# First attention layer, batches 0 and 1: row maxima read from the PSUM banks, scores formed a second time, negated maxima added by TensorE

## The chip, the core and the metric

The kernel is one program on one core of a Trainium2 chip. Its time is the device time of one execution in microseconds (us), median over runs. [...]

## The reference, cut to what matters

Four layers are chained with residual additions: an attention over the sequence with shared queries, keys and values and a mask, a second attention with modulated normalisation, a long scan of 256 steps, and a recurrent cell. Everything is fp32. Only the first layer is touched:

```python
qh = q.reshape(B, T, NH, dk).transpose(0, 2, 1, 3)      # B=8, T=512, NH=8, dk=32
scores = scale * jnp.einsum('bhqd,bhkd->bhqk', qh, qh)
logits = (scores * cmask + (1.0 - cmask) * NEG) * rmask
attn = jax.nn.softmax(logits, axis=-1)
ctx = jnp.einsum('bhqk,bhkd->bhqd', attn, qh)
```

## The kernel before

**Units.** The first layer of a batch `b` is cut into eight units `(b, e, kc)`: `e` is one of two groups of four heads, `kc` one of four blocks of 128 keys. A unit is four score tiles of 128 keys x 512 queries, one per head of the group. Because queries and keys are the same projection, the score matrix is symmetric, and the maximum along a row is also the maximum of a column.

**What a unit goes through.** `scores0` lets TensorE form the four tiles in four PSUM banks (L224: contraction over 32 rows, so the four heads use four row strips of the array) and ScalarE copies them to the SBUF tile `sc` (L229, four copies). `maxima0` (L234) is one VectorE reduction over 128 x 2048 that writes four columns of the tile `mxp0`. When all four `kc` of a group are reduced, `rows0` transposes `mxp0` on TensorE (L241), copies the result to `mrow` (L243), writes it to DRAM in four small DMAs (L247) and reads it back, broadcast to all 128 partitions, as `bc` (L248, 1 MB). `weights0` (L252) is one VectorE subtraction of `bc` from `sc`, `exps0` (L256) one ScalarE exponential over 128 x 2048 whose bias is the key mask. `values0` (L267) multiplies with the values and with ones into two further banks; `weigh0` (L284, L285 on VectorE, then GpSimd) divides. `masked_out` (L294, L297) is the output projection of the batch.

**Order.** All of it is emitted by a hand-written loop over steps `g`, with no scheduler: in step `g`, batch `b` forms the scores of unit `i` at `g = 8b-4+i`, runs `rows0` at `g = 8b` and `8b+4` (the very first group at `g = -1`), forms the weights of unit `i` at `g = 8b+1+i` and the values at `g = 8b+2+i`. Within a step the order is `scores0`, `rows0`, `project` (L198), `values0`, `project_out` (L215), `modulate` (L322, L325), `weights0` and `exps0`, `mask` (L210), `weigh0`, `maxima0`, `masked_out`, `modulation` (L153, steps 3 to 6), `normalize` (L306 to L311, batch 0 in step 11) and `qkv` (L334, batch 0 from step 13). From step 20 the heads of the second layer run as well. That layer already uses the scheme that the change brings to the first: `maxima1` reduces out of the banks (L393), `weights1` forms the scores again (L407) and adds negated maxima with a matrix `pick` (L417), and the exponential reads the bank (L427).

**Banks.** `bank(...)` hands out the five PSUM banks of the pool `ps_s`, to scores, projections, transposes and `qkv` alike. A freed bank goes to the end of a queue: the next request takes the bank whose last reader comes earliest in the program, and TensorE waits there until that reader is done. The values have banks of their own.

Of the kernel before, what the change touches and what calls it, by code (L numbers as in the profile page):

```python
# [8 lines left out]
F32 = mybir.dt.float32  # L9
AF = mybir.ActivationFunctionType  # L10
ALU = mybir.AluOpType
AX = mybir.AxisListType
# [3 lines left out]
P = 128  # L16
# [9 lines left out]
def attention(ctx, tc, cst, x, cond, wqT, woT, w_emb, b_emb, g_norm, w_qkv, g_q, g_k, w_out, follow):  # L26
# [14 lines left out]
    nc = tc.nc  # L41
# [4 lines left out]
    DH = 32  # L46
    SC = 1.0 / math.sqrt(DH)
    U = 8

    wp = ctx.enter_context(tc.tile_pool(name="a_w", bufs=1))  # L50
    big = ctx.enter_context(tc.tile_pool(name="a_big", bufs=1))
# [9 lines left out]
    def bank(shape, name):  # L61
        return ps_s.tile(shape, F32, tag="s", name=name)
# [60 lines left out]
    mxp0 = fone.tile([P, P], F32, name="mxp0")  # L123
    mxp1 = wp.tile([P, P], F32, name="mxp1")

    pick = wp.tile([P, 2, P], F32, name="pick")
    nc.gpsimd.memset(pick, 0.0)
    for h in range(4):
        for q in range(2):
            nc.gpsimd.tensor_tensor(  # L130
                pick[:, q, :], pick[:, q, :], ident[:, 32 * h + q : 32 * h + q + 1].to_broadcast([P, P]), ALU.add
            )
# [55 lines left out]
        nc.vector.tensor_mul(out, pc[:, 0, :], r)  # L188


    qms, psqs, qtoks, means, scs, bcs, pc0s, ctxTs = {}, {}, {}, {}, {}, {}, {}, {}

    def project(b, e):
        if e == 0:
# [23 lines left out]
    def scores0(b, e, kc):  # L218

        qm = qms[b, e]  # L220
        ss = [bank([P, D], f"s0_{b}_{e}_{kc}_{h}") for h in range(4)]
        for h in range(4):
            r = 32 * h
            nc.tensor.matmul(  # L224
                ss[h], lhsT=qm[r : r + 32, kc * P : (kc + 1) * P], rhs=qm[r : r + 32, :], start=True, stop=True
            )
        sc = ftwo.tile([P, 4, D], F32, tag="sc", name=f"sc_{b}_{e}_{kc}", bufs=7)
        for h in range(4):
            nc.scalar.copy(sc[:, h, :], ss[h])  # L229
        scs[b, e, kc] = sc  # L230

    def maxima0(b, e, qc):

        nc.vector.tensor_reduce(  # L234
            mxp0.rearrange("p (h i) -> p h i", i=32)[:, :, qc], scs[b, e, qc], AX.X, ALU.max
        )

    def rows0(b, e):

        pt = bank([P, P], f"pm0_{b}_{e}")  # L240
        nc.tensor.transpose(pt, mxp0, ident)  # L241
        mrow = ftwo.tile([P, P], F32, tag="mrow", name=f"mrow0_{b}_{e}", bufs=1)
        nc.scalar.copy(mrow, pt)  # L243
        bc = bcs[b, e] = ftwo.tile([P, 4, D], F32, tag="bc", name=f"bc_{b}_{e}")
        row = dram.tile([4, D], F32, tag="row", name=f"row_{b}_{e}", bufs=2)
        for h in range(4):
            nc.sync.dma_start(row[h].rearrange("(q n) -> q n", n=P), mrow[32 * h : 32 * h + 4, :])  # L247
        nc.sync.dma_start(bc, row.rearrange("h n -> (h n)").partition_broadcast(P).rearrange("p (h n) -> p h n", h=4))  # L248

    def weights0(b, e, kc):  # L250
        sc = scs[b, e, kc]
        nc.vector.tensor_sub(sc, sc, bcs[b, e])  # L252

    def exps0(b, e, kc):
        sc = scs[b, e, kc]
        nc.scalar.activation(sc, sc, AF.Exp, bias=negT[:, kc, b : b + 1], scale=SC)  # L256

# [39 lines left out]
            nc.vector.tensor_add(xs[b][:, m, :], ps, xs[b][:, m, :])  # L297


    xhs, xnTs, qTs, kTs, vts, mrows1, exs1, oTs = {}, {}, {}, {}, {}, {}, {}, {}  # L300

    def normalize(b):
        ss = sm.tile([P, 2], F32, tag="ss", name=f"ss_{b}")
        xh = [line(f"xh_{b}_{m}") for m in range(2)]
        for m in range(2):
            nc.scalar.activation(xh[m], xs[b][:, m, :], AF.Square, accum_out=ss[:, m : m + 1])  # L306
        rr = sm.tile([P, 2], F32, tag="rr", name=f"rr_{b}")
        nc.gpsimd.tensor_scalar(rr, ss, 1.0 / D, EPS, ALU.mult, ALU.add)
        nc.gpsimd.tensor_tensor(rr, rr, mhalf[:, 0:2], ALU.pow)
        for m in range(2):  # L310
            nc.scalar.activation(xh[m], xs[b][:, m, :], AF.Copy, scale=rr[:, m : m + 1])  # L311
        xhs[b] = xh

    def modulate(b):
        xnT = xnTs[b] = big.tile([P, NJ, 256], F32, tag="xnT", name=f"xnT_{b}")
# [180 lines left out]
    def leave(kind):  # L496
        for key in [k for k in left if k[0] == kind]:
            yield *key[1:], left.pop(key)

    with tc.manual_schedule():  # L500
        for g in range(-5, OUT[-1][1] + 1):

            a0, v0 = at(g, -4, U), at(g, 2, U)
            w1, v1 = heads(g, 1), heads(g, 2)

            a1, early = heads(g, 1, range(B - 2)), heads(g, 0, range(B - 2, B))
            late = a1 is not None or heads(g, 0, range(B - 2)) is not None
            turns, turned = list(leave("qkv")), list(leave("qt"))
            if a1:
                maxima1(*a1)  # L510
                if v1:
                    values1(*v1)
                if a := due.pop("weigh", None):
                    weigh0(*a)
            elif a0:
                scores0(a0[0], a0[1] // 4, a0[1] % 4)
            if (a := at(g, -3, U)) and a[1] % 4 == 3 and g > 0 and not a1:
                rows0(a[0], a[1] // 4)

            pr = at(g, -5, 2)  # L520
            if pr and not late:
                project(*pr)
            if v0 and not late:
                values0(v0[0], v0[1] // 4, v0[1] % 4)
            for a in turned:
                project_out(*a)
            if g == OUT[-1][1]:
                cst["soon"]()
                scan_start(cst["pool"], nc, cst)
            if g - 1 in norms:  # L530
                modulate(norms.index(g - 1))
            if a1 and a0:
                scores0(a0[0], a0[1] // 4, a0[1] % 4)
            if (a := at(g, -3, U)) and a[1] % 4 == 3 and a1:
                rows0(a[0], a[1] // 4)
            if w1:
                rows1(*w1)
            if e0 := at(g, 1, U):
                weights0(e0[0], e0[1] // 4, e0[1] % 4)
                if not late:  # L540
                    exps0(e0[0], e0[1] // 4, e0[1] % 4)
            if pr and not late:
                mask(*pr)
            if v0 and not late and v0[1] % 4 == 3:
                weigh0(v0[0], v0[1] // 4)
            if a0 and a0[1] % 4 < 3:
                maxima0(a0[0], a0[1] // 4, a0[1] % 4)

            if pr and late:
                project(*pr)  # L550
                mask(*pr)
            if a := at(g, U + 2):
                masked_out(a[0])
            if 3 <= g < 7:
                modulation(2 * g - 6)
            if g == U:
                scale_shift()
                add_identity()
            if g in norms:
                normalize(norms.index(g))  # L560
            made = [(part, qkv(*part)) for part in parts.get(g, ())]
            for b in range(B):
                for half in range(2):
                    if OUT[b][half] == g:
                        modulated_out(b, half)
                    if OUT[b][half] == g and (b, half) == (B - 1, 0):
                        for s in range(4):
                            for m in range(NJ // 2):
                                drive_of(nc, cst["us"], cst["x2T"], cst["ubias"], 0, s, m)
            if a0 and a0[1] % 4 == 3:  # L570
                maxima0(a0[0], a0[1] // 4, 3)
            if g == -1:
                rows0(0, 0)
            for part, lines in made:
                if lines:
                    qkv_norm(*part, *lines)
                    left["qkv", *part] = lines[1]
            if not w1:
                for a in turns:
                    qkv_out(*a)  # L580
            if early:
                maxima1(*early)

            if v1 and not a1:
                values1(*v1)
            if w1:
                weights1(*w1)
                for a in turns:
                    qkv_out(*a)
            if e0 and late:  # L590
                exps0(e0[0], e0[1] // 4, e0[1] % 4)
            if v0 and late:
                values0(v0[0], v0[1] // 4, v0[1] % 4)
                if v0[1] % 4 == 3:
                    due["weigh"] = v0[0], v0[1] // 4
            if (a2 := at(g, -7)) and a2[0] > 1:
                load(a2[0])
            if g == -1:
                load_weights()
            if g == U * B + 2:  # L600
                first.close()
                follow()
                for (b, half), d in x2d.items():
                    nc.sync.dma_start(
                        cst["x2T"][:, 2 * half : 2 * half + 2, b, :], d.rearrange("p (m t) -> p m t", m=2)
                    )
# [645 lines left out]
```

## Time and profile before

| | us |
|---|---|
| median of 3 runs | 2793.96 (2788.45 to 2795.03) |
| profiled execution, device time | 2791.91 |
| its span in the profile | 2790.0 |
| TensorE busy | 2709.0 (97%) |
| VectorE busy | 2130.1 (76%) |
| ScalarE busy | 1665.1 (60%) |
| GpSimd busy | 1247.9 (45%) |

The attention layers take about the first quarter of the span, the scan and the recurrent cell the rest. The change concerns steps -4 to 16, the first 153 us. TensorE's share over the whole span says little about these: in the 78 us from the start of step 3 (42.21 us) to that of step 13 (120.31 us) it is busy for 59.01 us. In the rows below, a line such as L224 is a line of the kernel before; PE is TensorE, DVE is VectorE, ACT is ScalarE, POOL is GpSimd, SP the engine that issues the DMAs. In a timeline row the numbers are start, duration, then engine, line, operation and tile, and in brackets how long the engine had been idle and what ended that. An fp32 matmul counts as two instructions there.

### The profile page before, as it was taken

The page shows a single profiled execution, that of the slowest core. Times are in us where ns is not written, and L with a number is a line of the kernel's source. Part 1 is how long each engine was busy: PE and PEld are TensorE (multiplying, and loading weights), DVE is VectorE, ACT ScalarE, POOL GpSimd, SP SyncE. Part 2 cuts the span into 40 slices and gives each one's busy share as a digit, 9 for nine tenths or more (in the row PEclk, how much of TensorE's full clock was granted, in tenths as well). Part 3 has the DMA queues.
Part 4 walks back from the last instruction along what each step waited for, and adds up shares of the span by engine and source line. Part 5 has one row for each costly group of instructions (what it writes and reads, how often), then busy time and mean ns, then how long its engine had stood idle before and what let it go on. Part 6 is the DMA issues. An engine that isn't in the chain of part 4 may idle for free.

```text
span 2790.0 us, 168552 instructions
## 1 busy us (share of the span) xinstructions
PE 2709.0 (97%) x71862; PEld 2063.7 (74%) x71862; DVE 2130.1 (76%) x9290; ACT 1665.1 (60%) x8176; POOL 1247.9 (45%) x3605
## 2 busy tenths in 40 slices
PE   7799999999989999999999999999999999999999
PEld 3234445444567888888888888888888888888888
DVE  6767776775347888888888888888888888888887
ACT  5666666664336666666666666666666666666653
POOL 1144323433314555555555545555555555544554
PEclk8899999999999999999999999999999999999999
DMA  4111101110400000000000000000000000000000
GB/s 152 42 43 35 43 24 50 35 35 20 151 2 4 7 7 8 7 7 7 7 7 7 7 7 7 7 7 7 8 8 7 7 7 7 7 7 7 7 7 8
DMA packets 56819, 58.17 MB, mean 21 GB/s; under 512 B 42832, under 2 KB 46456, under 8 KB 54016
## 3 DMA queue, kind: packets, MB, share of 16 engines
q1 hardware_dynamic: 55984, 47.39, 5.3%
q8 instruction: 561, 9.19, 1.4%
q14 instruction: 194, 1.59, 0.2%
q10 hardware_dynamic: 80, 0.01, 0.0%
HBM read 40.15 MB, written 7.21 MB: 17 GB/s over the span
## 4 chain that ended last, share of the span: by engine, by line
PE 89%; ACT 5%; DVE 3%; POOL 2%; issue 1%; DMA 1%; SPq 0%; DVEq 0%; ACTq 0%; POOLq 0%
PE ic L821 36%; PE pg L852 16%; PE gi L834 8%; PE pn L852 8%; PE psqkv L334 6%; PE pc L267 3%; PE pc L177 2%; PE s L224 2%; PE psx L453 1%; PE s L407 1%; PE n L385 1%; PE pso L294 1%; ACT sc L229 1%; PE s L417 1%; ACT sc L256 1%; PE psq L198 1%
## 5 line engine op out<-in xcount | busy, mean ns | idle before, releaser
L821 PE MATMUL ic<-cT_sb,tT 128*8 128x128 f32 x32736 | 1086.9, 273 | 9.5 <-ACT tT L719 8.8
L821 PEld LDWEIGHTS ic<-cT_sb,tT 128*8 128x8 f32 x32736 | 758.2, 89 | 254.8 <-ACT tT L719 213.2
L719 ACT ACTIVATE tT<-qn 128x16 f32<-128x16 f32 x2046 | 439.6, 215 | 548.2 <-DVE qn L1150 510.7
L1141 DVE STREAM_TRANSPOSE icT<-ic 128x64 f32<-128x64 f32 x2048 | 504.6, 246 | 55.1 <-PE ic L821 31.6
L852 PE MATMUL pg<-whh_sb,hz 128*32 128x128 f32 x16064 | 534.1, 273 | 0.0
L816 POOL TENSOR_TENSOR W<-W,cx 128x128 f32<-128x128 f32 x765 | 297.6, 389 | 375.3 <-ACT cx L792 371.8
L852 PEld LDWEIGHTS pg<-whh_sb,hz 128*32 128x32 f32 x16064 | 451.1, 110 | 1.5 <-issue 0.8
L1150 DVE SCALAR_TENSOR_TENSOR qn<-icT,hqs 128x16 f32<-128x16 f32 x2048 | 350.0, 171 | 70.1
L806 POOL TENSOR_TENSOR W<-cx,us 128x128 f32<-128x128 f32 x255 | 116.7, 457 | 433.4 <-ACT cx L792 433.4
L834 PE MATMUL gi<-wih_sb,x3T 128*32 128x128 f32 x8256 | 275.0, 274 | 0.0
L852 PE MATMUL pn<-whh_sb,hz 128*32 128x128 f32 x8032 | 267.8, 273 | 0.0
L834 PEld LDWEIGHTS gi<-wih_sb,x3T 128*32 128x32 f32 x8256 | 224.2, 110 | 16.8 <-POOL x3T L1164 16.6
L852 PEld LDWEIGHTS pn<-whh_sb,hz 128*32 128x32 f32 x8032 | 226.0, 110 | 1.0 <-issue 0.5
L1098 DVE SCALAR_TENSOR_TENSOR sqmm<-sqmm,qn 128x32 f32<-128x32 f32 x768 | 142.8, 186 | 97.6 <-ACT sqmm L1081 97.5
L1107 DVE TENSOR_TENSOR hqs<-W,sqmm 128x32 f32<-128x32 f32 x1020 | 194.7, 191 | 18.6 <-DVE sqmm L1098 0.5
L792 ACT ACTIVATE cx<-qn 128x32 f32<-128x32 f32 x1280 | 200.6, 213 | 0.0
L792 ACT ACTIVATE cx<-p 128x32 f32<-128x32 f32 x1020 | 149.9, 217 | 53.5 <-DVE p L1093 53.5
L334 PE MATMUL psqkv<-wqkv_sb,xnT 128*128 128x512 f32 x384 | 175.5, 603 | 3.8 <-ACT sc L229 3.1
L234 DVE TENSOR_REDUCE mxp<-sc 128x4 f32<-128x2048 f32 x64 | 145.9, 2282 | 26.4 <-ACT sc L229 26.2
L393 DVE TENSOR_REDUCE mxp<-n 128x2 f32<-128x512 f32 x128 | 79.5, 683 | 109.9 <-PE n L385 109.9
L229 ACT COPY sc<-s 128x512 f32<-128x512 f32 x256 | 131.4, 608 | 42.2 <-PE s L224 42.2
L252 DVE TENSOR_TENSOR sc<-sc,bc 128x2048 f32<-128x2048 f32 x64 | 147.5, 2305 | 11.7 <-DMA bc<-row 11.7
(176 smaller groups left out, 3875.3 us busy)
## 6 DMA issues: line engine op xcount, KB each, us to landing
bc<-row SPq DMA_DIRECT2D x16, 1024.0 KB
out<-o SPq DMA_DIRECT2D x1008, 4.0 KB
x<-in_x SPq DMA_DIRECT2D x8, 512.0 KB
wqkv_sb<-in_L_cond_W_qkv SPq DMA_DIRECT2D x1, 3072.0 KB
wih_sb<-in_L_cond_W_ih SPq DMA_DIRECT2D x4, 768.0 KB
whh_sb<-in_L_cond_W_hh SPq DMA_DIRECT2D x4, 768.0 KB
x2d<-x2o SPq DMA_DIRECT2D x11, 256.0 KB
x2T<-x2d SPq DMA_DIRECT2D x11, 256.0 KB
```

The costliest lines, as they stand in the source:

```text
L229: nc.scalar.copy(sc[:, h, :], ss[h])
L252: nc.vector.tensor_sub(sc, sc, bcs[b, e])
L334: nc.tensor.matmul(ps, lhsT=xnTs[b][:, c, m * P : (m + 1) * P], rhs=wqkv_sb[:, c, part * D : (part + 1) * D], start=(c == 0), stop=(c == N ...
L719: seen["tanh"] = nc.scalar.activation(tT, src[:, half * HM : (half + 1) * HM, :], AF.Tanh)
L792: a = nc.scalar.activation(c[:, i], x, AF.Copy, scale=f)
L816: seen["sum"] = nc.gpsimd.tensor_tensor(W[:, i + 1 : 5], W[:, i + 1 : 5], c, ALU.add)
L821: last = nc.tensor.matmul(ps[32 * j : 32 * j + B, :], lhsT=tT[k // HM][:, k % HM, :], rhs=cT_sb[:, k, 0, :, j, :], start=(k == 0), stop=(k ...
L834: nc.tensor.matmul(gi_ps[rows(j), g, :], lhsT=x3T[c][:, k, :], rhs=wih_sb[:, k, g, :, j, :], start=(k == 0), stop=(k == NJ - 1),)
L852: nc.tensor.matmul((pg_ps, pg_ps, pn_ps)[g][rows(j), :], lhsT=hzs[tau % 3][:, k, 32 * (g % 2) : 32 * (g % 2) + 32], rhs=whh_sb[:, k, g, :, ...
L1107: nc.vector.tensor_sub(hq, W[:, s], mm)
L1141: turn = nc.vector.transpose(icT.rearrange("p m n -> p (m n)"), ic[:, half * 64 : half * 64 + 64])
L1150: stt(qn[:, m2, :], icT[:, :, 0:B], IC[s], hq[:, m2, :], ALU.mult, ALU.add)
```

## The change

For batches 0 and 1 (`DIRECT = 2`):

- `scores0` no longer copies; VectorE reduces each of the four banks straight into a column of `mxp0`. These reductions stand at the place of `scores0`, at the head of the step, while the one of `maxima0` stood near its end.
- `rows0` ends with a ScalarE copy scaled by -1 into `nrow`; the DRAM round trip is gone.
- `weights0` asks for four banks again, forms the scores again and adds `-max` with 16 small matmuls (`pick` gets four planes instead of two); ScalarE takes the exponential from the banks, four times 128 x 512.
- `maxima0` and `exps0` do nothing for these batches. `mrow` has two buffers.
- `normalize` of batch 0 is split: the two scaled copies stand at the head of step 12 instead of in step 11.

```diff
+    DIRECT = 2
...
-    pick = wp.tile([P, 2, P], F32, name="pick")
+    pick = wp.tile([P, 4, P], F32, name="pick")
...
-        for q in range(2):
+        for q in range(4):
...
     def scores0(b, e, kc):
...
+        if b < DIRECT:
+            for h in range(4):
+                nc.vector.tensor_reduce(mxp0[:, 32 * h + kc : 32 * h + kc + 1], ss[h], AX.X, ALU.max)
+            return
...
     def rows0(b, e):
...
+        if b < DIRECT:
+            nrows[b, e] = ftwo.tile([P, P], F32, tag="mrow", name=f"nrow_{b}_{e}", bufs=2)
+            nc.scalar.activation(nrows[b, e], pt, AF.Copy, scale=-1.0)
+            return
...
     def weights0(b, e, kc):
+        if b < DIRECT:
+            qm, nrow = qms[b, e], nrows[b, e]
+            ss = [bank([P, D], f"w0_{b}_{e}_{kc}_{h}") for h in range(4)]
+            for h in range(4):
+                r = 32 * h
+                nc.tensor.matmul(
+                    ss[h], lhsT=qm[r : r + 32, kc * P : (kc + 1) * P], rhs=qm[r : r + 32, :], start=True, stop=False
+                )
+            for q in range(4):
+                for h in range(4):
+                    r = 32 * h
+                    nc.tensor.matmul(
+                        ss[h][:, q * P : (q + 1) * P],
+                        lhsT=pick[r : r + 4, q, :],
+                        rhs=nrow[r : r + 4, :],
+                        start=False,
+                        stop=(q == 3),
+                    )
+            sc = scs[b, e, kc] = ftwo.tile([P, 4, D], F32, tag="sc", name=f"sc_{b}_{e}_{kc}", bufs=7)
+            for h in range(4):
+                nc.scalar.activation(sc[:, h, :], ss[h], AF.Exp, bias=negT[:, kc, b : b + 1], scale=SC)
+            return
...
     def normalize(b):
...
+        if b > 0:
+            normalized(b)
+
+    def normalized(b):
         for m in range(2):
-            nc.scalar.activation(xh[m], xs[b][:, m, :], AF.Copy, scale=rr[:, m : m + 1])
+            nc.scalar.activation(xhs[b][m], xs[b][:, m, :], AF.Copy, scale=rrs[b][:, m : m + 1])
...
+            if g - 1 == norms[0]:
+                normalized(0)
```

More of the change, by code (lines that the diff above doesn't have):

```diff
@@ L188, in weigh @@
         nc.vector.tensor_mul(out, pc[:, 0, :], r)
-    qms, psqs, qtoks, means, scs, bcs, pc0s, ctxTs = {}, {}, {}, {}, {}, {}, {}, {}
+    qms, psqs, qtoks, means, scs, bcs, nrows, pc0s, ctxTs = {}, {}, {}, {}, {}, {}, {}, {}, {}
     def project(b, e):
@@ L241, in rows0 @@
         nc.tensor.transpose(pt, mxp0, ident)
-        mrow = ftwo.tile([P, P], F32, tag="mrow", name=f"mrow0_{b}_{e}", bufs=1)
+        if b < DIRECT:
+            nrows[b, e] = ftwo.tile([P, P], F32, tag="mrow", name=f"nrow_{b}_{e}", bufs=2)
+            nc.scalar.activation(nrows[b, e], pt, AF.Copy, scale=-1.0)
+            return
+        mrow = ftwo.tile([P, P], F32, tag="mrow", name=f"mrow0_{b}_{e}", bufs=2)
         nc.scalar.copy(mrow, pt)
@@ L250, in weights0 @@
     def weights0(b, e, kc):
+        if b < DIRECT:
+            qm, nrow = qms[b, e], nrows[b, e]
[18 more added lines that the diff above has]
+                nc.scalar.activation(sc[:, h, :], ss[h], AF.Exp, bias=negT[:, kc, b : b + 1], scale=SC)
+            return
         sc = scs[b, e, kc]
@@ L254, in exps0 @@
     def exps0(b, e, kc):
+        if b < DIRECT:
+            return
         sc = scs[b, e, kc]
@@ L297, in masked_out @@
             nc.vector.tensor_add(xs[b][:, m, :], ps, xs[b][:, m, :])
-    xhs, xnTs, qTs, kTs, vts, mrows1, exs1, oTs = {}, {}, {}, {}, {}, {}, {}, {}
+    rrs, xhs, xnTs, qTs, kTs, vts, mrows1, exs1, oTs = {}, {}, {}, {}, {}, {}, {}, {}, {}
     def normalize(b):
@@ L309, in normalize @@
         nc.gpsimd.tensor_tensor(rr, rr, mhalf[:, 0:2], ALU.pow)
+        xhs[b] = xh
+        rrs[b] = rr
+        if b > 0:
+            normalized(b)
+    def normalized(b):
         for m in range(2):
-            nc.scalar.activation(xh[m], xs[b][:, m, :], AF.Copy, scale=rr[:, m : m + 1])
-        xhs[b] = xh
+            nc.scalar.activation(xhs[b][m], xs[b][:, m, :], AF.Copy, scale=rrs[b][:, m : m + 1])
     def modulate(b):
```

## The prediction

> **What bounds the kernel now.** I read the chain of work that ended last over the first 300 us, then the waits of the first 200 us, the timeline of steps -4 to 18, and for prices the groups by shape and the second layer, which already works in the new way.
>
> The chain shows two regimes. Up to step 12 it runs through DMA round trips and whatever VectorE has to do behind them; from step 13 it is TensorE alone:
>
> ```profile
> 29.59 4.63 DMA bc<-row
> ...
> 54.86 4.69 DMA bc<-row
> ...
> 82.17 5.06 DMA bc<-row
> 87.25 2.29 DVE sc L252
> ...
> 138.05 1.07 PE s L224 x8
> 139.12 1.85 PE pc L267 x16
> 140.98 3.65 PE psqkv L334 x8
> ```
>
> The last three rows add to 6.57 us, and that is a whole step: scores start at 137.98 (step 15) and 144.54 (step 16). There every matmul added lengthens the step. The timeline gives the start of the scores in steps 3 to 17: 42.2, 49.2, 57.0, 62.2, 71.5, 76.5, 79.7, 83.7, 100.8, 106.3, 120.3, 131.4, 138.0, 144.5, 153.0.
>
> The waits say what the round trip costs: 10.6 us of VectorE idle in five waits, of which batches 0 and 1 have four (0.91, 3.00, 3.73, 1.26 in the timeline, sum 8.9). TensorE's longest wait is a consequence, for VectorE is late with `weigh0`:
>
> ```profile
> DVE sc L252 <- DMA bc<-row: 10.6, 5, 3.7
> PE pc L267 <- DVE ctxT L285: 12.0, 2, 9.1
> ```
>
> From 42.2 to 120.3 us (steps 3 to 12) the busy times by window give TensorE 59.0 of 78.1 us: 19.1 us idle.
>
> **Prices.** Groups of the page (mean ns is the figure after the busy time):
>
> ```profile
> L234 DVE TENSOR_REDUCE mxp<-sc 128x4 f32<-128x2048 f32 x64 | 145.9, 2282 | 26.4 <-ACT sc L229 26.2
> L393 DVE TENSOR_REDUCE mxp<-n 128x2 f32<-128x512 f32 x128 | 79.5, 683 | 109.9 <-PE n L385 109.9
> L229 ACT COPY sc<-s 128x512 f32<-128x512 f32 x256 | 131.4, 608 | 42.2 <-PE s L224 42.2
> L252 DVE TENSOR_TENSOR sc<-sc,bc 128x2048 f32<-128x2048 f32 x64 | 147.5, 2305 | 11.7 <-DMA bc<-row 11.7
> ```
>
> The second layer, first as the chain, then as the timeline:
>
> ```profile
> 668.85 0.65 PE s L407 x8
> 669.49 0.45 PE s L417 x16
> ```
>
> ```profile
> 670.90 2.06 ACT L427 ACTIVATE ex<-s 128x512 f32<-128x512 f32 x4 [1.43 <-PE s L417]
> 673.77 2.49 DVE L393 TENSOR_REDUCE mxp<-n 128x2 f32<-128x512 f32 x4 [3.54 <-PE n L385]
> 676.31 0.33 PE L397 MATMUL pm<-ident,mxp 128*128 128x128 f32 x1 [0.69 <-DVE mxp L393]
> ```
>
> Per unit the change removes four copies (2.05 us in a row at 131 us) and an exponential of 2.00 from ScalarE, and gives it four exponentials (2.06, second row): -2.0. VectorE loses 2.28 + 2.31 and gets four reductions from the banks, 2.49 in a row: -2.1. TensorE gets a second score block, 1.07, and 16 small matmuls: eight took 0.45 (chain row), so 0.90. Four rows of `pick` instead of two is not in the trace; if the strips did not overlap it would be 16 times two 0.27 us rows, 8.6, but L417 shows them overlapped, so 0.90, and twice that at the half clock. Together +1.97 for each of 16 units.
>
> At no cost: eight more `pick` additions on GpSimd (2.89 us for eight now, over by 9.3 us, first use near 32 us). The 20 DMAs go from SP's queue, so `wqkv_sb` and `wout_sb`, queued behind the first `bc` at 29.98, leave earlier; their cover is that they are first read in step 13 and step 8. Without it they would delay `x` of batch 1, needed at 43 us; that one is queued ahead. The split `normalize` leaves ScalarE's order as it was, as nothing of ScalarE stands between the two places.
>
> **The new waits.** Now each unit passes the five banks twice, and what TensorE waits for is read off the order of requests.
>
> Scores behind weights. In steps without other work behind `weights0`, the next scores get banks that the exponentials still read. The third one ends 0.1 + 3 x 0.515 = 1.65 us after the last small matmul. A late bank costs a full matmul more:
>
> ```profile
> 100.78 1.83 PE L224 MATMUL s<-qm 32*128 32x512 f32 x8
> 101.50 0.29 PEld L224 LDWEIGHTS s<-qm 32*128 32x128 f32 x2 [0.41 <-DVE x L297]
> ```
>
> From 101.50 to 102.61 is 1.11. So such scores end 2.75 after, instead of 1.07: +1.7 in steps 3, 8, 9, 10; where it is the fourth exponential, +2.2 in steps 12 and 13, +0.3 in step 5.
>
> `rows0` behind reductions. In steps 4 and 8 the four reductions of the next group are issued ahead of the transposition of `mxp0`, which they write too. TensorE waits for them in order, and `project` and `values0` stand behind it: +2.5 (2.49 above) in step 4, and 0.7 in step 8, where the staggered scores hide the rest.
>
> `modulation` in step 3 asks for the banks of exponentials just issued: +1.2.
>
> Step by step, from the TensorE rows (scores 1.07, values 1.85, weights 1.97, projection 1.95, transposes 0.6, `modulation` 1.86, `masked_out` 3.63) and these waits:
>
> - step 3: 2.75 + 1.95 + 1.85 + 1.97 + 1.2 + 1.86 + 0.1 = 11.7 (6.9 before); 4: 12.2 (7.8); 5: 7.7 (5.2); 6: 6.9 (9.4); 7: 5.0 (4.9)
> - step 8: 2.75 + 0.7 + 0.33 + 1.85 + 1.97 = 7.6 (3.3); 9: 6.6 (4.0); 10: 10.2 (17.1); 11: 6.9 (5.5)
> - step 12: 19.0 (14.0). `normalize` stays exposed: the exponentials now end 2.2 into the step, squares 1.3, GpSimd 2.9, the copies to the projection's bank 1.85, then as before 7.2 to the end of the transposes (the projection at half clock, 3.78), 1.65 for `xnT`, whose banks the weights get, 1.1 and 0.9.
>
> Sum 93.8 against 78.1: **+15.7**. Checked from the other side: without any wait the TensorE rows of these steps add to 71.7, so 22.1 of it are waits.
>
> Steps 13 to 16: +0.2 (step 13 was slow before, at half clock), +2.0, +2.0, +1.0 (a wait for GpSimd of 0.84 in step 16 is covered): **+5.2**.
>
> Start: 16 reductions in a row end at 24.8 instead of 26.4, and no round trip follows, but scores and weights take turns in the banks: step 3 starts at 39.8 at full clock, 43.2 at half (the window 30 to 40 us shows 0.50 now), taken 41.5: **-0.7**, bounds -2.4 and +1.0.
>
> Sum +20.2. Nothing after step 17 differs, and its waits are relative to TensorE's place, so it is carried to the end: 2791.91 + 20.2 = 2812.1. The median stands 2.05 above the profiled execution: **2814**.
>
> **The clock.** The rows show the half rate after idle times:
>
> ```profile
> 81.84 1.06 PE L267 MATMUL pc<-sc,qtok 128*32 128x512 f32 x8 [0.94 <-ACT sc L256]
> 93.94 1.94 PE L267 MATMUL pc<-sc,qtok 128*32 128x512 f32 x8 [9.10 <-DVE ctxT L285]
> 123.90 1.86 PE L267 MATMUL pc<-sc,qtok 128*32 128x512 f32 x8 [1.68 <-ACT sc L256]
> ```
>
> 0.94 leaves full speed, 1.68 does not, and one such episode costs 1.4 to 1.8 us (3.5 to 3.8 for the pair of rows instead of 2.1; 3.78 instead of 1.98 for a projection). The new waits of 1.7 to 2.5 lie on that edge. I leave them at full clock, since work on both sides is dense.
>
> [...]
>
> **Rivals.**
> - *Clock falls at each bank wait.* 1.6 us in steps 3, 4, 5, 8, 9, 10 and 1.7 at the start: +11.3, **2825**. For: 123.90; against: 81.84.
> - *Engines run ahead.* ScalarE and VectorE have spare time, so two thirds of the 22.1 us of waits vanish: -14.7, **2799**. For: their busy time falls by 2 us a unit; against: TensorE's order is fixed and the bank needs its reader.
> - *Faster: the added matmuls fall into TensorE's idle time.* 10 units add 19.7 us in steps 3 to 12, where 19.1 are idle. If they fit, the round trip's 8.9 and the half-clock excess 8.1 go, and 5.2 of steps 13 to 16 stay: -11.8, **2782**. It decides if steps 7 to 9 stay near 5 us, that is if scores need not wait for exponentials. Against: five banks for eight tiles.
>
> **Numbers.** Forecast 0.66, clock 0.12, running ahead 0.13, faster 0.09. Range 2791 to 2832: from below the second rival to above the clock one with the start at its bad end. A measurement here tells 0.3%, 8.4 us, from no change: faster 0.09, same 0.13, slower 0.78.
>
> **What would show it.** Right: scores of step 17 near 173 us; steps 8 and 9 near 7 us, with L225 waiting for ScalarE's L282; in step 4 the transposition waiting 2.5 us for VectorE; steps 14 and 15 at 8.5. Wrong: step 3 to 13 in less than 80 us, or 14 and 15 still at 6.6.

## The result, and the profile after

The changed kernel takes 2824.66 us (median of 4 runs, 2823.02 to 2834.99); before, beside it, took 2791.65 (2788.45 to 2795.03). The ratio is 1.0131, 95% interval 1.0115 to 1.0148: it is slower, by 33 us by the medians and 37 by the ratio, where 20 were forecast. The profiled span is 2821.2 us, 31.2 more than before's 2790.0. From here on "step n" is the stretch from the start of step n's scores to that of step n+1.

On the page, TensorE has 50.9 us more busy time than before, of which 31.5 were forecast as added rows; VectorE has 31 less.

```profile
PE 2759.9 (98%) x72502; PEld 2095.9 (74%) x72502; DVE 2099.1 (74%) x9322; ACT 1642.6 (58%) x8160; POOL 1250.1 (44%) x3613
```

In the waits of the first 200 us (engine, line, what it waited for, total, times, longest) the two round-trip lines that the prediction showed are gone. ScalarE and VectorE now wait for TensorE's matmuls, and TensorE waits for VectorE's reductions, in step 4 for 2.65 us:

```profile
ACT sc L282 <- PE w L273: 54.2, 15, 9.5
DVE mxp L230 <- PE s L225: 36.0, 15, 5.3
...
PE pm L248 <- DVE mxp L230: 5.3, 3, 2.6
```

The chain that ended last (start, length, what), formerly DMA and VectorE up to step 12, is TensorE nearly throughout. The first four rows are the end of step 9 and the start of step 10: second scores, small matmuls, and then scores that last 3.09 instead of 1.07 us, because they wait for banks that the exponentials still read. The last five are step 15, the old 6.57 us plus 1.07 and 0.89:

```profile
105.19 1.07 PE w L267 x8
106.26 0.89 PE w L273 x32
107.15 3.09 PE s L225 x8
110.25 1.85 PE pc L302 x16
...
163.92 1.07 PE s L225 x8
164.99 1.85 PE pc L302 x16
166.84 1.07 PE w L267 x8
167.91 0.89 PE w L273 x32
168.81 3.64 PE psqkv L374 x8
```

Step 4 in the timeline (start, duration, line, tile; in brackets the idle time and what ended it) shows the costliest stretch. Scores run at half speed (2.09), the transposition waits 2.65 us for the last reduction, and the projection behind it is still at half speed (3.62 instead of 1.98):

```profile
53.90 2.09 PE L225 MATMUL s<-qm 32*128 32x512 f32 x8
56.01 2.49 DVE L230 TENSOR_REDUCE mxp<-s 128x1 f32<-128x512 f32 x4 [3.97 <-PE s L225]
58.64 0.44 PE L248 MATMUL pm<-ident,mxp 128*128 128x128 f32 x1 [2.65 <-DVE mxp L230]
58.88 3.62 PE L199 MATMUL psq<-x,wq_sb 128*128 128x512 f32 x4
```

The clock had already fallen when that wait began. Windows of 1 us (length, then the busy share of TensorE, of its weight loads, of VectorE, ScalarE and GpSimd; the granted clock is the third number from the end) put the fall at 53.3 us. A second one follows at 70.4 us, where TensorE has been counted busy without a pause since 58.6:

```profile
53.00:54.00 1.00, 1.00 (x11) 0.98 (x10) 0.00 (x0) 0.28 (x1) 0.00 (x0) 0.64 0.00 0
70.00:71.00 1.00, 1.00 (x9) 0.27 (x8) 0.00 (x0) 0.40 (x1) 0.00 (x0) 0.68 0.00 0
```

| stretch | before | forecast | after |
|---|---|---|---|
| start of step 3 | 42.21 | 41.5 | 41.90 |
| steps 3 to 12 | 78.10 | 93.8 | 100.06 |
| of these: 4, 5, 8 | 7.84, 5.20, 3.25 | 12.2, 7.7, 7.6 | 16.1, 9.0, 9.4 |
| steps 13 to 16 | 32.70 | 37.9 | 39.78 |
| start of step 17 | 153.01 | 173.2 | 181.74 |

### The profile page after: what moved, and what is told of

It is laid out like the page before. It is cut to its first block, busy times and chain, and to the rows that moved or that the text cites. A ratio compares the mean times of both kernels' runs of the same rounds, so it can differ in the third digit from the quotient of the medians.

```text
span 2821.2 us, 169835 instructions
## 1 busy us (share of the span) xinstructions
PE 2759.9 (98%) x72502; PEld 2095.9 (74%) x72502; DVE 2099.1 (74%) x9322; ACT 1642.6 (58%) x8160; POOL 1250.1 (44%) x3613
## 4 chain that ended last, share of the span: by engine, by line
PE 91%; ACT 4%; DVE 3%; POOL 1%; issue 1%; DMA 0%; SPq 0%; DVEq 0%; ACTq 0%; POOLq 0%
PE ic L863 35%; PE pg L894 15%; PE gi L876 8%; PE pn L894 8%; PE psqkv L374 6%; PE pc L302 4%; PE s L225 3%; PE pc L178 2%; PE psx L493 1%; PE s L447 1%; PE n L425 1%; PE s L457 1%; PE pso L329 1%; PE psq L199 1%; ACT sc L234 1%
## 5 line engine op out<-in xcount | busy, mean ns | idle before, releaser
L863 PE MATMUL ic<-cT_sb,tT 128*8 128x128 f32 x32736 | 1086.0, 273 | 9.9 <-ACT tT L761 9.1
L863 PEld LDWEIGHTS ic<-cT_sb,tT 128*8 128x8 f32 x32736 | 757.6, 89 | 255.9 <-ACT tT L761 215.4
L876 PEld LDWEIGHTS gi<-wih_sb,x3T 128*32 128x32 f32 x8256 | 224.2, 110 | 17.6 <-POOL x3T L1206 17.6
L834 ACT ACTIVATE cx<-q 128x32 f32<-128x32 f32 x1020 | 145.6, 213 | 0.0
L1123 ACT ACTIVATE sqmm<-qn 128x32 f32<-128x32 f32 x768 | 140.3, 183 | 0.0
L374 PEld LDWEIGHTS psqkv<-wqkv_sb,xnT 128*128 128x128 f32 x384 | 70.4, 191 | 91.5 <-issue 75.5
```

What stands on the lines that cost most here:

```text
L374: nc.tensor.matmul(ps, lhsT=xnTs[b][:, c, m * P : (m + 1) * P], rhs=wqkv_sb[:, c, part * D : (part + 1) * D], start=(c == 0), stop=(c == N ...
L834: a = nc.scalar.activation(c[:, i], x, AF.Copy, scale=f)
L863: last = nc.tensor.matmul(ps[32 * j : 32 * j + B, :], lhsT=tT[k // HM][:, k % HM, :], rhs=cT_sb[:, k, 0, :, j, :], start=(k == 0), stop=(k ...
L876: nc.tensor.matmul(gi_ps[rows(j), g, :], lhsT=x3T[c][:, k, :], rhs=wih_sb[:, k, g, :, j, :], start=(k == 0), stop=(k == NJ - 1),)
L1123: nc.scalar.activation(sq, qs, AF.Square, scale=math.sqrt(CUB[s]))
```

## The experiments

All ratios are to the kernel before. Beside each stands the start of step 17 in its one profiled execution; from there to the end the kernels are alike, but the stretch took 2633.2 to 2640.7 us in the traces, so a single span is not good to better than some us.

| run | ratio (95%) | median us | step 17 at |
|---|---|---|---|
| before | 1 | 2787.5 to 2791.7 | 153.0 |
| after | 1.0131 (1.0115 to 1.0148) | 2824.66 | 181.7 |
| e1 matmuls added, unread | 1.0084 (1.0069 to 1.0099) | 2812.96 | 172.6 |
| e2 no round trip | 0.9986 (0.9976 to 0.9996) | 2785.27 | 151.8 |
| e3 both | 1.0058 (1.0043 to 1.0073) | 2804.61 | 167.2 |
| e4 second tile of maxima | 1.0131 (1.0116 to 1.0146) | 2826.42 | 190.7 |
| e5 sums behind second scores | 1.0135 (1.0113 to 1.0157) | 2828.75 | 192.2 |
| e6 no small matmuls | 1.0054 (1.0036 to 1.0073) | 2805.30 | 167.1 |
| e7 e4, `modulation` in halves | 1.0134 (1.0116 to 1.0152) | 2827.54 | 192.7 |
| e8 three orders | 1.0117 (1.0099 to 1.0134) | 2822.57 | 180.0 |
| e9 one unit only | 0.9979 (0.9971 to 0.9988) | 2782.02 | 147.0 |
| e10 first blocks only | 1.0001 (0.9992 to 1.0010) | 2788.33 | 153.3 |
| e11 two orders | 1.0091 (1.0077 to 1.0105) | 2812.61 | 176.6 |
| e12 fillers | 1.0117 (1.0100 to 1.0134) | 2820.60 | 188.5 |

**The parts by themselves (e1, e2, e3).** e1 puts the second scores and small matmuls of the same shapes into before, at the place of `weights0`, into banks that nothing reads:

```diff
     def weights0(b, e, kc):
+        if b < 2:
+            qm = qms[b, e]
+            ss = [bank([P, D], f"w0_{b}_{e}_{kc}_{h}") for h in range(4)]
...
         sc = scs[b, e, kc]
         nc.vector.tensor_sub(sc, sc, bcs[b, e])
```

> The kernel before, with the added TensorE work of the change but without its handover: for batches 0 and 1 the second score block and the 16 small matmuls are issued at the place of the weights into four banks that nobody reads; everything else is as before. Theory A (banks changing hands, the ordered wait for the reductions and the half clock make most of the loss; the matmuls themselves fall largely into TensorE's idle time): +2 in each of steps 3 and 4, +7 in steps 13 to 16, nearly nothing in steps 5 to 12, in all +9 to +15 us against before. Rival B (the 16 x 1.97 = 31.5 us of added matmuls are the loss, since that is about what was measured): +28 to +33 us.

The ratio makes 23 us (0.0084 x 2789) of 31.5 us of rows, between the ranges of theory A and rival B and in neither. In steps 3 to 12 it is 15.2 of the ten units' 19.7 (93.33 against 78.10 us): only 4.5 vanish in idle time. TensorE's longest wait is still there, merely cut from 9.10 to 4.95 us, since its end is set by `bc` and then by VectorE's queue, neither of which the rows touch:

```profile
95.85 2.29 DVE L252 TENSOR_TENSOR sc<-sc,bc 128x2048 f32<-128x2048 f32 x1 [3.17 <-DMA bc<-row]
...
102.53 1.94 PE L285 MATMUL pc<-sc,qtok 128*32 128x512 f32 x8 [4.95 <-DVE ctxT L303]
```

e2 leaves the round trip out and subtracts a constant tile:

```diff
+        if b < 2:
+            if (b, e) == (0, 0):
+                bcs[0, 0] = fixed = ftwo.tile([P, 4, D], F32, tag="bc", name="bc_fixed")
+                nc.gpsimd.memset(fixed, 0.0)
+            bcs[b, e] = bcs[0, 0]
+            return
```

> The kernel before, without the DRAM round trip of the maxima for batches 0 and 1: the subtraction takes a constant tile, so the subtracted maxima are left out there; reductions, transposition and the copy to mrow stay. It prices what the change could win at most by dropping the trip. Theory A: the exposed 8.9 us of VectorE waits go, and part of the half-clock excess: -9 to -17 us against before. Rival C (the trip is hidden behind the chain of VectorE and TensorE, another wait takes its place): 0 to -4 us.

It gives 4 us (1 to 7), as rival C has it, where VectorE had waited 8.9. In step 9 the subtraction no longer waits, yet `weigh0` is still behind it, and step 10's values wait 5.17 us for VectorE instead of 9.10:

```profile
83.97 2.29 DVE L258 TENSOR_TENSOR sc<-sc,bc_fixed 128x2048 f32<-128x2048 f32 x1
...
86.17 1.75 DVE L290 RECIPROCAL r<-pc 128x256 f32<-128x256 f32 x1
...
90.64 1.93 PE L273 MATMUL pc<-sc,qtok 128*32 128x512 f32 x8 [5.17 <-DVE ctxT L291]
```

e3 is both edits at once.

> Both of the two others at once: no round trip (maxima not subtracted for batches 0 and 1) and the added matmuls into unread banks. This has the TensorE work of the changed kernel and no DMA wait, but ScalarE and VectorE work as before and no bank that must be read before TensorE goes on with the second block. Theory A: between -4 and +8 us against before, some 25 to 35 below the changed kernel. Rival B: +20 us or more, near the changed kernel.

16 us (12 to 20), again between theory and rival. So of the change's 37 us by ratio, 16 are there without any reader on the new banks. By subtraction about 20 are left for the readers: reductions and exponentials from banks, the handover, and what falls of the clock come with them.

**The small matmuls (e6).** Without them the maxima are not subtracted:

```diff
-            for q in range(4):
-                for h in range(4):
-                    r = 32 * h
-                    nc.tensor.matmul(
-                        ss[h][:, q * P : (q + 1) * P],
...
```

> The changed kernel without the 16 small matmuls of each unit: the maxima are not subtracted (that part of the computation is left out), all else is as it was. Theory P (TensorE's path is the sum of its rows): 16 units by 0.90 us, 14.4 us, and with the falls of the clock behind small matmuls up to 18: 2807 to 2811. Rival H (the exponentials' reads set when the next scores begin, but the exponentials only start 0.9 us earlier too, so nothing is hidden): the same 14. Rival W (the waits for reductions and banks take its place): only the 4 units of steps 13 to 16 and a few others gain, 6 to 9 us, 2816 to 2819.

1.0054 against 1.0131: 21 us by the ratios, 19 by the medians, for 14.4 us of rows, a little more than theory P expects. Up to step 17 its profile is 14.7 us ahead, 4.1 of them before step 3, 7.6 in steps 3 to 12 and 3.0 in steps 13 to 16; but from 42 to 200 us it is at half clock for some 7 us more than after, so the 14.7 are not the rows alone. The rows cost about their price or more, nothing hides them, and rival W falls.

**The wait of the transposition (e4, e12).** e4 gives the second group a maxima tile of its own, so that the transposition does not wait for the next group's reductions:

```diff
-                nc.vector.tensor_reduce(mxp0[:, 32 * h + kc : 32 * h + kc + 1], ss[h], AX.X, ALU.max)
+                nc.vector.tensor_reduce((mxp0, mxp1)[e][:, 32 * h + kc : 32 * h + kc + 1], ss[h], AX.X, ALU.max)
```

> The changed kernel with two tiles for the maxima (the second group of a batch uses the tile of the second layer, idle then), so that the transposition in steps 4 and 8 no longer waits for the next group's reductions. Theory A: the wait of 2.6 us in step 4 goes but for 0.6 (the projection asks for the first reduced bank), 0.8 goes in step 8, and some half clock with them: -3 to -7 us against the changed kernel, so +25 to +29 against before. Rival B: no change, +31 to +33 against before.

Nothing is gained: rival B's "no change". Step 4 does shrink from 16.1 to 13.7 us, its wait from 2.65 to 0.36, and step 8 from 9.4 to 7.1, but steps 6, 7, 9 and 10 grow by 1.9, 2.9, 3.0 and 3.1 us: from 42 to 200 us the clock is at half for some 51 us, against some 31 in after. In step 4 it is still at half, from 55.8 to 62.6 us, and the projection is as slow as in after with next to no wait ahead of it. So the wait does not set off that fall:

```profile
55.77 2.09 PE L225 MATMUL s<-qm 32*128 32x512 f32 x8
...
58.62 3.78 PE L199 MATMUL psq<-x,wq_sb 128*128 128x512 f32 x4 [0.36 <-DVE mxp L230]
```

Most of e4's falls come where TensorE is counted busy without a pause. Windows of 1 us of e4 (as above), with the timeline of the same place:

```profile
78.00:79.00 1.00, 1.00 (x12) 0.79 (x12) 0.43 (x2) 1.00 (x2) 0.45 (x1) 1.00 0.00 0
79.00:80.00 1.00, 1.00 (x12) 0.16 (x8) 0.43 (x1) 0.04 (x1) 0.92 (x2) 0.84 0.00 0
80.00:81.00 1.00, 1.00 (x8) 0.21 (x4) 1.00 (x3) 0.00 (x0) 1.00 (x1) 0.50 0.00 0
```

```profile
75.53 1.07 PE L273 MATMUL w<-nrow,pick 4*128 4x128 f32 x32
76.53 1.95 PE L154 MATMUL pe<-condT,wemb 128*128 128x8 f32 x16
78.41 1.22 PE L225 MATMUL s<-qm 32*128 32x512 f32 x8
79.56 1.89 PE L302 MATMUL pc<-sc,qtok 128*32 128x512 f32 x8
```

Shortly ahead of the fall, at 79.7 us, stand three microseconds of small matmuls (4 rows) and `modulation` (8 columns). e7 was to show that they are the cause:

```diff
-                modulation(2 * g - 6)
+                modulation(2 * g - 6, 1)
...
+            if 3 <= g < 7:
+                modulation(2 * g - 6, 0)
             pr = at(g, -5, 2)
```

> The kernel with a second tile of maxima (e4, 2826.4 us), with `modulation` of steps 3 to 6 issued in two halves, 8 narrow matmuls between scores and values and 8 at their old place behind the small matmuls of `weights0`. Theory N (stretches of narrow matmuls of about 3 us, 1.07 of small ones and 1.95 of `modulation`, let the clock fall though TensorE is busy): the half clock at 69 to 73, 79 to 84 and 86 to 94 us of e4 goes, 4 to 8 us less, 2818 to 2822. Rival I (the clock falls at idle time alone): nothing changes, 2825 to 2828.

It does not: the clock is at half from 54 to 61, 68 to 75, 82 to 85 and 89 to 95 us, and the time is what it was. Theory N, as put, falls. Rival I has the number but not the reason, for these falls do not stand behind idle time: e7's TensorE has a busy share of 1.00 in every window of 1 us from 42 to 130 us. e12 fills the waits with full-size matmuls instead:

```diff
+        if n := {(0, 1): 3, (1, 0): 1, (1, 1): 6}.get((b, e)):
+            fl = bank([P, D], f"fill_{b}_{e}")
+            for i in range(n):
+                nc.tensor.matmul(fl, lhsT=wq_sb[:, 0, 0:P], rhs=xs[1][:, 0, :], start=True, stop=True)
         nc.tensor.transpose(pt, mxp0, ident)
```

> The changed kernel with full-size matmuls whose result is not read, put ahead of the transposition of the maxima, where TensorE waits for the reductions: 3 in step 4 (1 us each at full clock, in a wait of 2.65 us), 1 in step 8, 6 in step 12 (in the wait for `normalize`). Theory C (idle TensorE in the wait is what holds the clock at half): in step 4 the projection behind takes 2.0 instead of 3.62 us and the values 2.1 instead of 2.6; in step 8 the values 2.1 instead of 3.4; in step 12 the projection 2.0 instead of 3.78: 3 to 6 us less than the changed kernel's 2824.7, that is 2819 to 2822. Rival (the fall is set ahead of the wait, at 53.4 in step 4, and the added rows only lengthen the path): 2824 to 2828.

Where they stand, they do what theory C says: in step 4 the half clock ends at 57.5 instead of 63.5 us and the projection takes 1.88 instead of 3.62 us; in step 12, 1.88 instead of 3.78. The fall in step 4 is there all the same, at 54.1 us and ahead of the wait, as the rival says: filling the wait only shortens it, from 10.2 to 3.4 us. And step 12 gets longer, 19.0 us instead of 17.6, for the six matmuls let the projection start 10.3 us into the step instead of 6.9.

```profile
53.80 1.87 PE L225 MATMUL s<-qm 32*128 32x512 f32 x8
55.59 3.77 PE L250 MATMUL fill<-x,wq_sb 128*128 128x512 f32 x6
59.20 0.27 PE L252 MATMUL pm<-ident,mxp 128*128 128x128 f32 x1
59.31 1.88 PE L199 MATMUL psq<-x,wq_sb 128*128 128x512 f32 x4
```

For the whole it says little: the median lies 4 us under after's, where theory C has it, but the two intervals overlap, and the profiled execution had other falls (68 to 75, 78 to 85, 88 to 95 us) and reached step 17 later.

**The handover of the banks (e5, e8, e11).** Half of the values, the matmuls with ones, moves between the second scores and the next scores, so that both wait less for readers:

```diff
             if v0 and not late:
-                values0(v0[0], v0[1] // 4, v0[1] % 4)
+                values0(v0[0], v0[1] // 4, v0[1] % 4, (0,) if v0[0] < 2 else (0, 1))
...
+            if v0 and not late and v0[0] < 2:
+                values0(v0[0], v0[1] // 4, v0[1] % 4, (1,))
             if pr and not late:
                 mask(*pr)
```

> The changed kernel, with the half of the values' matmuls that forms the sums (0.9 us a step, batches 0 and 1) issued behind the second scores instead of ahead of them, so that the next scores come 0.9 us later and the second scores 0.9 us earlier. Theory H (the banks' handover: scores wait for the exponentials' last reads, some 1.7 us in steps 3, 8, 9, 10 and 2.2 in 12 and 13): 7 to 11 us less than the changed kernel's 2824.7, that is 2814 to 2818. Rival C (what the waits cost beyond TensorE's added rows is the half clock): the falls of the clock stay, and no more than 3 us go, 2822 to 2826.

A miss: no gain, 2828.75 us, above both ranges. e8 adds to it the transposition ahead of the next scores (`rows0` moved to the head of the step) and `modulation` in halves:

```diff
+            if (a := at(g, -3, U)) and a[1] % 4 == 3 and g > 0 and a[0] < DIRECT:
+                rows0(a[0], a[1] // 4)
             if a1:
                 maxima1(*a1)
```

> The changed kernel with three changes of order: the transposition of the maxima ahead of the next scores (so it waits for no reductions of the next group), the sums' half of the values behind the second scores, and `modulation` in two halves. If handover and clock are what made up the waits: 14 to 20 us less than the changed kernel, 2805 to 2811. If TensorE's added rows are all that counts: 0 to 4 us less. It should not come below the kernel before, since the rows that are added in steps 13 to 16 alone are worth 5 us and the round trip that they replace at most 4 (e2).

Also a miss, in the range for "TensorE's added rows are all that counts", but its timeline says more. Steps 3 to 9 take 56.7 us instead of 65.1, and step 10 takes 17.5 instead of 10.65: since the sums now come late in step 9, `weigh0` starts late, VectorE has it ahead of the reductions, and both step 10's values and second scores wait for that. From 105.0 to 115.2 us the clock is at half as well, and `masked_out` takes 5.69 us instead of 3.70. Steps 14 to 16 take 0.8 to 0.9 us more each.

```profile
99.42 1.76 DVE L319 RECIPROCAL r<-pc 128x256 f32<-128x256 f32 x1 [2.55 <-PE pc L302]
...
103.67 2.48 DVE L230 TENSOR_REDUCE mxp<-s 128x1 f32<-128x512 f32 x4
103.81 1.06 PE L302 MATMUL pc<-sc,qtok 128*32 128x512 f32 x8 [2.36 <-DVE ctxT L320]
...
111.17 5.69 PE L329 MATMUL pso<-ctxT,wo_sb 128*128 128x512 f32 x8
```

e11 keeps the two orders and moves the sums only where no `weigh0` follows, up to step 12:

```diff
-                values0(v0[0], v0[1] // 4, v0[1] % 4)
+                values0(v0[0], v0[1] // 4, v0[1] % 4, (0,) if g < 13 and v0[1] % 4 < 3 else (0, 1))
```

> The changed kernel with the transposition of the maxima ahead of the next scores, and the sums' half of the values behind the second scores only up to step 12 and only where no `weigh0` follows (in e8 `weigh0` was so pushed into step 10, which took 17.5 us instead of 10.65, and steps 14 to 16 took 0.9 us more each). `modulation` is in its old place. Theory: e8's gains in steps 3 to 9 stay (some 8 us) and its losses go (6.9 and 2.6): 2809 to 2814. Rival (something else is late next and gives it all back): 2820 to 2825.

2812.61, inside the expectation: 1.0091 against 1.0131, intervals apart, some 11 us of the change's 37 taken back by order alone. The number came in, the account behind it only in part. Steps 3 to 9 take 54.8 us instead of 65.1, and steps 14 to 16 what they take in after. But step 10 still takes 17.2 us, though `weigh0` now starts ahead of it: TensorE is counted busy throughout, at half clock from 101.1 to 114.8 us. So what lengthened step 10 in e8 was not `weigh0` alone, and that e11 met its range is partly luck: more was gained ahead of step 10 than expected, and one of the two losses stayed.

```profile
97.52 1.76 DVE L319 RECIPROCAL r<-pc 128x256 f32<-128x256 f32 x1 [0.45 <-PE pc L302]
...
99.23 4.22 PE L225 MATMUL s<-qm 32*128 32x512 f32 x8
...
110.84 5.64 PE L329 MATMUL pso<-ctxT,wo_sb 128*128 128x512 f32 x8
```

In the profiled executions step 17 starts 5.1 us earlier than in after; another 4.3 us lie in the stretch behind it, which varies by as much from trace to trace. Step 4 is at full clock throughout and takes 10.1 us instead of 16.1, with neither wait nor fall:

```profile
52.62 1.95 PE L154 MATMUL pe<-condT,wemb 128*128 128x8 f32 x16
54.42 0.31 PE L248 MATMUL pm<-ident,mxp 128*128 128x128 f32 x1
54.66 1.14 PE L225 MATMUL s<-qm 32*128 32x512 f32 x8
55.73 1.98 PE L199 MATMUL psq<-x,wq_sb 128*128 128x512 f32 x4
```

**A version that beats both (e9, e10).** The rows cost least where TensorE idles most: step 9's weights, behind which step 10's 9.10 us of waiting stand. e9 is before with the new way for that unit alone; `mrow` is negated and `bc` added. The unit's subtraction, which waits for `bc` ahead of `weigh0`, goes from VectorE's queue with it:

```diff
         sc = scs[b, e, kc]
-        nc.vector.tensor_sub(sc, sc, bcs[b, e])
+        if (b, e, kc) == (1, 0, 0):
+            qm, nrow = qms[b, e], nrows[b, e]
...
+            for h in range(4):
+                nc.scalar.activation(sc[:, h, :], ss[h], AF.Exp, bias=negT[:, kc, b : b + 1], scale=SC)
+            return
+        nc.vector.tensor_add(sc, sc, bcs[b, e])
```

> The kernel before with the second scores for a single unit, the first key block of batch 1's first group (weights of step 9); the other 15 units keep the subtraction of `bc`, now an addition of negated maxima. In before, step 9's subtraction waits 3.73 us for `bc` (to 87.25), and `weigh0`, queued behind it on VectorE, releases the values' bank at 93.8, for which TensorE waits 9.1 us. Theory V (the exit of step 9 is VectorE's queue; 2 us more on TensorE lie in its idle time): `weigh0` starts at about 84, step 10's values at 88 to 90 instead of 93.94, 4 to 7 us less than before. Rival M (the wait moves: second scores wait for banks, or step 10's values wait for exponentials): 0 to 2 us less.

0.9979 (0.9971 to 0.9988), 6 us less, as expected. The gain comes from VectorE's queue; the added rows use up part of TensorE's wait. `weigh0` starts at 84.15 instead of 89.46, and step 10's values at 89.02 instead of 93.94, at full clock; step 9 grows by 1.9 us and step 10 falls from 17.1 to 8.6:

```profile
84.02 1.14 PE L258 MATMUL w<-qm 32*128 32x512 f32 x8
84.15 1.76 DVE L308 RECIPROCAL r<-pc 128x256 f32<-128x256 f32 x1 [0.32 <-PE pc L291]
84.98 1.07 PE L264 MATMUL w<-mrow,pick 4*128 4x128 f32 x32
...
89.02 1.07 PE L291 MATMUL pc<-sc,qtok 128*32 128x512 f32 x8
```

e10 does the same for the first block of all four groups:

```diff
-        if (b, e, kc) == (1, 0, 0):
+        if b < 2 and kc == 0:
```

> As e9, for the first key block of all four groups of batches 0 and 1 (weights of steps 1, 5, 9 and 13), that is for the units that stand behind a round trip. Theory V: what e9 gives, and in step 5 some 1 us more (`weigh0` can start at 60.0 instead of 61.8, against 2.0 us of rows on TensorE), in step 13 about nothing, at the start up to 2 us: 5 to 9 us less than before. Rival R (TensorE's rows count where the waits are short): the three other units cost 1 to 2 us each, so 1 to 3 us less than before in all, or none.

The gain is gone (1.0001): step 3 starts 2.5 us later than before, step 13 takes 13.2 instead of 11.1, and step 10 falls back to half clock, from 88.9 to 95.7 us. Rival R holds in the sum, but not unit by unit: steps 5 to 7, behind step 5's second scores, take 16.8 us instead of before's 19.5. A kernel with step 5's and step 9's unit was not tried.

## Why the prediction was right, and where its size was off

- **The bound.** Two regimes were read, and steps 14 and 15, where every row counts, took 8.52 us each: forecast 8.5, +2.0 each.
- **Rows against idle time.** The forecast put the added 1.97 us a unit on the path. e1 shows it for most of them: of 19.7 us in steps 3 to 12 only 4.5 are absorbed, because the idle time is bunched behind VectorE's queue, in step 10 above all, and rows elsewhere cannot use it. That is why the faster rival fell; e9, with its rows in that very gap and one subtraction less in VectorE's queue, shows that it was right there.
- **The round trip.** The 8.9 us of waits have no line of their own in the sum; they go inside the steps (step 10 was forecast at 10.2 us instead of 17.1 and took 10.65). By itself the trip is worth 4 us (e2).
- **The waits.** Scores behind exponentials: +1.7 was forecast for steps 9 and 10; the scores last 3.1 us instead of 1.07, so +2.0, and the steps took 6.9 and 10.65 (6.6 and 10.2 forecast). The exponentials from banks were 2.42 us for four, not the 2.06 of the second layer's row. `rows0` behind reductions: +2.5 forecast, 2.65 measured. Rival "engines run ahead" fell: steps 3 to 12 took 100.06 us, and in step 4 the projection stood behind the transposition's 2.65 us; but a changed order does take back 11 us (e11).
- **The term that was mis-sized: the clock, left at full speed.** "I leave them at full clock, since work on both sides is dense" is what failed. Steps 4, 5 and 8 took 3.9, 1.3 and 1.8 us more than forecast, all three with matmul rows at half speed, and step 13 took 13.4 us instead of 11.3 with scores of 3.91 and values of 1.94 and 1.72. Steps 3 to 12 are 6.3 us over the forecast and 13 to 16 are 1.9 over; with 0.4 at the start and 2.5 behind step 17 that makes the 11 us by which the span is off. From 42 to 200 us before is at half clock for some 27 us and after for some 31: the falls in steps 6, 7 and 10 of before went, as the forecast has it, and others came in steps 4, 5 and 8.
- **What sets off the falls.** The prediction read an edge between 0.94 and 1.68 us of idle time out of three rows. A fourth row of before, in step 7, is at half speed behind 0.38 us:

```profile
73.05 1.93 PE L267 MATMUL pc<-sc,qtok 128*32 128x512 f32 x8 [0.38 <-ACT sc L256]
```

In after, steps 3, 9 and 10 wait 2 us for banks (scores of 3.21, 3.27 and 3.27 us in the timeline, 1.14 where they do not wait) and stay at full clock, the fall in step 4, at 53.3 us, begins ahead of the wait of 2.65 us, and the one in step 5, at 70.4 us, has no wait ahead of it. Both follow small matmuls and `modulation` (1.07 and 2.21 us, 1.97 and 1.95 us). The fall in step 8, at 94.3 us, lies in 0.82 us of idle time, behind scores that waited for banks (the last seven of the eight took 2.78 us). e4 has the fall of step 4 without that wait, and in e12, which fills it, the half clock lasts 3.4 us instead of 10.2. In e11 wait and fall are both gone, but there the values' matmuls with ones (1.06 us) also stand between the small ones and `modulation`, so it does not tell the two apart. The rival that charged 11.3 us for falls at the bank waits met the median, 2825, by coincidence: of its six steps three stayed at full clock.
- **The signs.** The transposition's wait of 2.5 us (2.65), steps 14 and 15 at 8.5, step 9 near 7 (6.9) and scores that wait for the exponentials came as forecast. Step 8 near 7 us (9.4) and step 17 near 173 us (181.7) did not.
- **Step 12** took 17.6 us instead of 19.0. The chain shows `normalize` exposed, as forecast, with squares, GpSimd and copies from 125.2 to 131.2.
- **The tail.** "Carried to the end" is off by 2.5 us, which is within what that stretch varies from execution to execution.
- **Costed at nothing.** The longer `pick`, the split `normalize` and the DMAs taken from SP's queue were not tried apart; the start of step 3 (41.90 against 41.5) leaves no room for a large cost of the first.

## What to carry to other kernels

Idle time of an engine pays for added work only if the work stands in that very gap: find which queue ends the gap, relieve that queue, and put the rows there (one unit out of sixteen gained 6 us, all sixteen lost 37). When banks are handed from reader to reader, the order inside a step decides who waits, and an edit that frees one wait should be followed to the next queue and to the clock, as step 10 in e8 and e11 showed. Falls of the clock belong in such a sum as a term with a range, not as nothing: here they came in three steps that the forecast had at full clock, not in those with the most waiting for banks, and these three took 7 us more than forecast.

## What was not expected of the hardware

- In after, e4, e7 and e12 the granted clock falls at places where TensorE is counted busy without a break for ten microseconds and more: in after at 70.4 us (busy since 58.6), in e4 at 79.7 (since 58.6), in e7 at 68.0 (since 42 at least), in e12 at 67.7 (since 51.8). Part of the busy time in these runs is matmuls that wait for a bank (scores of 3.2 instead of 1.1 us) and part is very small matmuls; e7 did not settle which of them lets the clock fall. In e11, with the values' matmuls with ones between the small ones and `modulation`, the first fall in these steps comes at 80.7 us.
- The busy share does not tell where a fall follows. In windows of 1 us it is 1.00 ahead of after's falls at 53.3 and 70.4 us (52 to 53, 69 to 70), and it is 1.00 in e11 in every window from 47 to 80 us, where the granted clock is 1.00 too. In before it is 0.00 from 85 to 89 us at a granted clock of 1.00, and the fall comes at 89.9. Nor do matmuls of few columns by themselves: from 832 to 2821 us of after, where the matmuls of the scan use 8 columns of the array (L863, 273 ns each), the granted clock is 1.00. What sets off a fall was not shown.
- Falls can outweigh waits in a single execution: e4's profiled one, the slowest of its four, is at half clock for some 20 us more than after's (51 against 31), though e4 has the shorter waits.
